# Segment sums on one Trainium2 core: additions two products behind their matmuls, with PSUM banks redistributed

## The chip, the cores and the metric

The kernel runs on one core of a Trainium2 chip. The metric is the device time of one launch in microseconds. Nine runs before the change have a median of 2163.39 us (2159.84 to 2167.46).

The engines are named as in the profile: PE is TensorE, DVE VectorE, ACT ScalarE, POOL GpSimd, and SP is the engine whose queue issues most DMA transfers. PEld is PE's loading of weights.

## The reference

A graph layer with a residual and a layer norm. There are 6250 nodes and 206250 edges, all with 128 features in float32.

```python
edge_aggr = zeros((n, 128)).at[src].add(edge_attr)          # 206250 rows into 6250
combined  = concat([x, edge_aggr, repeat(global_feat, n)]) @ W_c + b_c
h = softplus(combined @ W1 + b1)
h = softplus(h @ W2 + b2)
out = layernorm(x + h @ W3 + b3)                            # no scale or shift
```

`src` is not sorted. Nearly all of the time goes to the scatter-add in the first line.

## The kernel before, in words

**The data.** An edge's row of 128 numbers lies on one partition, and 128 edges, one a partition, make a column: 1611 whole columns and one of 42 edges. The node sums are kept transposed in one tile, `sums_t`: 128 features on the partitions, 25 blocks of 256 nodes (`BL`) along the row.

**Two ways to add.** The first 48 columns (`DIRECT`) are added directly. ACT compares an edge's node with 512 node numbers at a time (`compare`, L535, two columns a step, tile `direct_hot`). PE multiplies the rows with these comparisons into the PSUM tile `direct_sum` (L552). After 12 columns DVE adds the bank to `sums_t` (L556).

All other edges go through buckets, in ten groups (`GROUPS`) of 40, 120, 200, 240, 240, 240, 212, 140, 88 and 44 columns. Each group has four stages:

- *Positions* (`positions`, L236): each edge gets a row in a DRAM table (`place`) in which edges of one node block lie together. A block's bucket is padded to whole chunks. DVE, PE and PSUM work this out: `count` and `count2` count edges by block (PSUM tile `small`, L261), `totals` makes bucket starts, `scan` counts along a partition, `place` sums it across partitions on PE (PSUM tile `pr`, L325 to L331), `place2` turns it into positions (L340, L342), and `chunk_map` writes each chunk's block as an offset (`offs`, L360).
- *Scatter* (`scatter_rows`, L601): SP loads pieces of ten columns (`rows`, five buffers, loaded three pieces ahead), ACT writes each edge's node number into its 129th element (`code_rows`, L599), and POOL scatters one column at a time with an indirect DMA (L607): 1564 of them.
- *Fill* (`fill_rows`): SP overwrites the table with -1 rows beforehand, so that padding matches no node.
- *Sums* (`reduce_steps`, L384): SP loads 1024 bucket rows at a time (`load`, tile `chunks`). DVE compares their node numbers with 256 numbers in one instruction (`match`, L406, tile `hot`). PE multiplies rows with comparisons (`total`, L421), 128 by 256, into a PSUM tile `part` of two sums. DVE adds each sum into `sums_t` at an offset that it has read into a register (L413 reads, L426 adds). A product, in the sense of this text, fills one `part` tile. A load makes four products in groups 0 and 9 (one row tile a sum), two in groups 1, 7 and 8 (two row tiles a sum) and one in the others (four).

**The order.** While group g is scattered, the sums of group g-1, the positions of group g+1 and the fill for group g+1 are done. Each engine's order is the order in which the Python code calls (a manual schedule for PE, DVE, ACT and SP), and every engine takes its instructions in that order. All SP transfers are in one order as well. For each piece the loop from L659 on issues a row load, a copy and ten scatters, and then as many steps of four lists as are due (`prep`, `sums`, `other`, `filled`): `AHEAD` says at which share of a group's pieces each list must be empty. `other` holds the node rows: `node_rows` (L443) turns x with PE (L489) and multiplies it by folded weights (L497), all of it during group 3, with two `x_sb` buffers. The direct steps are spread over groups 1 to 6 by `left` (L653).

In `reduce_steps`, step i loads chunk i+2, compares chunk i and then does the products and additions of chunk i-1. There are four chunk buffers, two comparison buffers and two `part` banks. The eight PSUM banks before are: one for `iota_ps`, two `small`, two `pr`, two `part`, one `direct_sum`.

**The end.** After the last group's scatter its sums are made (L689), and then two softplus layers, the last layer and the layer norm run over 13 tiles of up to 512 nodes (L702 on), with x loaded again by SP and b3 added to it on POOL (L796).

## Time and profile before

| | |
|---|---|
| median of nine runs | 2163.39 us |
| the profiled execution | 2164.55 us, span 2162.8 us |
| granted PE clock, mean | 0.917 |
| PE busy | 1766.1 us (82%) |
| DVE busy | 1383.4 us (64%) |
| ACT busy | 815.3 us (38%) |
| POOL busy | 1554.7 us (72%) |
| scatters (L607) | 1564, mean 958 ns, first at 26.6 us, last at 2006.0 us |
| matmuls of the bucket sums (L421) | 4472, mean 393 ns |
| comparisons of the buckets (L406) | 281, mean 2268 ns |
| additions (L426) | 781, mean 420 ns |

A span runs from the first to the last instruction; the profiled execution's own time is 1.75 us more. Times in the rows of the profile are microseconds from the span's start unless they are marked ns. "A <- B" in a list of waits means that A stood idle until B was done; the three numbers are the total, how often, and the longest. Register and semaphore instructions do not count as busy, and matmul ends are modelled. A float32 matmul shows as two instructions.

### The profile page before, as it was taken

The numbers are of one execution on the slowest core, as the hardware profiler recorded it, in microseconds if no ns is written. First come the engines' busy times: TensorE is split into PE (matmuls) and PEld (weight loads), VectorE is DVE, ScalarE is ACT, GpSimd is POOL, SyncE is SP. The second block draws the span as 40 slices with busy tenths as digits, with TensorE's granted clock in tenths as the row PEclk, the third lists the DMA queues.
The fourth block names the chain that finished last, engine by engine and source line by source line (L and its number), as shares of the span: only waits on it lengthen the run. The fifth ranks groups of instructions, "written<-read, shape, count | busy, mean of one in ns | idle before, by whom it ended". The sixth has DMA issues, their size and how long they took to land.

```text
span 2162.8 us, 22153 instructions
## 1 busy us (share of the span) xinstructions
PE 1766.1 (82%) x6415; PEld 1185.4 (55%) x6415; DVE 1383.4 (64%) x1943; ACT 815.3 (38%) x1174; POOL 1554.7 (72%) x1631
## 2 busy tenths in 40 slices
PE   3399798957999959999769998499983898688885
PEld 0144355534666636666446665276762777567653
DVE  7386476424777537776347764277662788798867
ACT  0367675652444444545443554443430000000035
POOL 5677777777777777777777777777777777777026
PEclk8699898977999979999979999799996999899997
DMA  9998788738888656566466555465654777777421
GB/s 291 303 323 268 211 252 251 241 101 255 240 255 237 179 149 216 189 207 209 131 184 202 185 180 183 133 207 193 202 185 147 213 229 228 199 215 204 122 77 60
DMA packets 415375, 435.49 MB, mean 201 GB/s; under 512 B 37743, under 2 KB 305766, under 8 KB 415254
## 3 DMA queue, kind: packets, MB, share of 16 engines
q1 hardware_dynamic: 365062, 330.71, 52.4%
q0 software_dynamic: 50048, 103.35, 14.3%
q8 instruction: 51, 0.84, 0.2%
q14 instruction: 70, 0.57, 0.1%
q10 hardware_dynamic: 144, 0.02, 0.0%
HBM read 260.90 MB, written 173.03 MB: 201 GB/s over the span
## 4 chain that ended last, share of the span: by engine, by line
PE 39%; POOL 18%; DMA 17%; issue 11%; DVE 10%; ACT 2%; SPq 2%; DVEq 0%; POOLq 0%; ACTq 0%
PE part L421 22%; POOL place L607 18%; PE direct_sum L552 13%; DMA place<-rows,pos 9%; DMA chunks<-place 4%; DVE sums_t L426 4%; DVE hot L406 2%; SPq L143 2%; DMA x_sb<-in_x 2%; DMA place<-fill 2%; DVE so_far L309 1%; DMA rows<-in_edge_attr 1%; PE pr L331 1%; ACT direct_hot L540 1%; PE small L266 1%
## 5 line engine op out<-in xcount | busy, mean ns | idle before, releaser
L607 POOL DMA_INDIRECT place<-rows,pos x1564 | 1497.9, 958 | 501.9 <-issue 445.8
L421 PE MATMUL part<-hot,chunks 128*128 128x256 f32 x4472 | 1062.2, 393 | 201.7 <-DVE hot L406 169.0
L421 PEld LDWEIGHTS part<-hot,chunks 128*128 128x128 f32 x4472 | 863.7, 196 | 421.7 <-DVE hot L406 187.0
L406 DVE SCALAR_TENSOR_TENSOR hot<-chunks,iota_ps 128x2048 f32<-128x2048 f32 (+1 forms) x281 | 637.1, 2268 | 259.9 <-DMA chunks<-place 259.9
L540 ACT ACTIVATE direct_hot<-iota_f,less 128x512 f32<-128x512 f32 (+1 forms) x624 | 405.1, 696 | 674.0 <-PE direct_sum L552 671.6
L552 PE MATMUL direct_sum<-direct_hot,direct_rows 128*128 128x512 f32 (+1 forms) x1248 | 581.6, 599 | 66.0 <-DMA direct_rows<-in_edge_attr 27.1
L426 DVE TENSOR_TENSOR sums_t<-sums_t,part 128x256 f32 x781 | 327.8, 420 | 334.6 <-PE part L421 313.0
L552 PEld LDWEIGHTS direct_sum<-direct_hot,direct_rows 128*128 128x128 f32 x1248 | 239.4, 196 | 284.6 <-issue 228.8
L542 ACT ACTIVATE direct_hot<-direct_hot,ones 128x1024 f32<-128x1024 f32 (+1 forms) x312 | 348.1, 1116 | 10.1
L599 ACT COPY rows<-low 128x10 f32<-128x10 f32 (+1 forms) x159 | 31.3, 199 | 514.9 <-DMA place<-rows,pos 474.6
L342 DVE TENSOR_REDUCE pos<-at 128x20 int32<-128x500 f32 (+2 forms) x80 | 87.1, 1089 | 2.7
L309 DVE TENSOR_TENSOR_SCAN so_far<-iota_ps,ib 128x1500 bf16<-128x1500 f32 (+5 forms) x29 | 85.7, 2955 | 0.0
L556 DVE TENSOR_TENSOR sums_t<-sums_t,direct_sum 128x512 f32<-128x512 f32 (+1 forms) x52 | 34.6, 666 | 66.7 <-PE direct_sum L552 65.9
L796 POOL TENSOR_TENSOR x_sb<-x_sb,b_all 128x512 f32<-128x512 f32 (+1 forms) x13 | 15.3, 1221 | 80.9 <-DMA x_sb<-in_x 80.9
L340 DVE TENSOR_TENSOR at<-pr,ib 128x500 f32<-128x500 f32 (+2 forms) x80 | 52.8, 659 | 3.0 <-PE pr L331 2.4
L721 ACT ACTIVATE away<-z_ps 128x512 f32<-128x512 f32 (+1 forms) x13 | 7.2, 554 | 120.3 <-PE z_ps L711 120.3
L784 POOL TENSOR_SCALAR y<-y,mv,rs 128x128 f32<-128x128 f32 (+1 forms) x45 | 35.1, 792 | 17.2 <-DVE rs L778 17.0
L255 DVE TENSOR_TENSOR ib<-block,iota_ps 128x1500 bf16<-128x1500 bf16 (+5 forms) x29 | 44.3, 1550 | 0.0
L266 PE MATMUL small<-ib,ones_h 128*128 128x500 bf16 (+2 forms) x80 | 24.2, 412 | 24.0 <-DVE ib L255 24.0
L327 PE MATMUL pr<-so_far,ones_h 128*128 128x500 bf16 (+2 forms) x80 | 32.2, 402 | 13.5 <-DVE last L312 13.5
L326 PE MATMUL pr<-ib,upto_h 128*128 128x500 bf16 (+2 forms) x80 | 32.1, 402 | 9.6 <-DVE at L340 9.6
L331 PE MATMUL pr<-begin,scale_h 2*128 2x500 bf16 (+2 forms) x80 | 32.6, 407 | 0.0
(113 smaller groups left out, 415.7 us busy)
## 6 DMA issues: line engine op xcount, KB each, us to landing
chunks<-place SPq DMA_DIRECT2D x278, 516.0 KB, 5.7
rows<-in_edge_attr SPq DMA_DIRECT2D x155, 640.0 KB, 5.1
place<-fill SPq DMA_DIRECT2D x252, 258.0 KB, 8.1
place<-rows,pos POOLq DMA_INDIRECT x1564, 4.3
x_sb<-in_x SPq DMA_DIRECT2D x24, 256.0 KB, 4.6
direct_rows<-in_edge_attr SPq DMA_DIRECT2D x4, 768.0 KB, 7.9
out<-y SPq DMA_DIRECT2D x12, 256.0 KB, 2.2
chunks<-place SPq DMA_DIRECT2D x3, 258.0 KB
```

Of the source, the lines that this page charges most:

```text
L266: nc.tensor.matmul(got["sum"][:, :, :j1 - j0], ones_h, in_block[k][1][:, :, j0:j1], start=(k == 0 and j0 == 0), stop=(k == len(parts) - 1 ...
L309: nc.vector.tensor_tensor_scan(t, iota_ps[:, 1:2].to_broadcast([P, NB * n]), in_block[k][0], 0.0, op0=ALU.mult, op1=ALU.add)
L331: nc.tensor.matmul(pr, scale_h, got["begin"].unsqueeze(2).to_broadcast([2, NB, m]), start=False, stop=True)
L340: nc.vector.tensor_mul(at, got.pop((k, j0)), in_block[k][1][:, :, j0:j1])
L342: nc.vector.tensor_reduce(pos[:, a - c0 + j0:a - c0 + j1], at.rearrange("p b g -> p g b"), axis=mybir.AxisListType.X, op=ALU.add)
L406: nc.vector.scalar_tensor_tensor(hot[:, :m], chunks[i][:, :m, D:W].to_broadcast([P, m, BL]), float(1 + BL * g), iota_ps.unsqueeze(1).to_br ...
L421: nc.tensor.matmul(part[:, s - q, :], t[:, s * sub + j, :D], hot[:, s * sub + j], start=(j == 0), stop=(j == sub - 1))
L426: nc.vector.tensor_add(here, here, part[:, s - q, :])
L540: nc.scalar.activation(hot[:, j, :n], iota_f[:, :n], AF.Abs, bias=less[:, w, c + q + j:c + q + j + 1], scale=-1.0)
L542: nc.scalar.activation(hot[:, :, :n], hot[:, :, :n], AF.Relu, bias=ones[:, :1], scale=-1.0)
L552: nc.tensor.matmul(sum_of[c, w][:, :n], rows_in[c][:, q + j, :], hot[:, j, :n], start=(q + j == 0), stop=(q + j == k - 1))
L607: s = nc.gpsimd.indirect_dma_start(out=dst, out_offset=bass.IndirectOffsetOnAxis(ap=at, axis=0), in_=rows[:r, j, :], in_offset=None)
```

## The change

- `reduce_steps`: `total` is split into `product` (matmuls of one `part` tile) and `add` (its additions). Step i loads chunk i+3, compares chunk i, and issues chunk i's products at once; after each product the oldest waiting additions are issued until only two products wait (`SUMS` - 1). The register load of a chunk's offsets stands before the chunk's first addition. A last step issues what still waits. There are three `part` banks, three comparison buffers (`hots`) and five chunk buffers.
- `place` takes its PSUM tile from the two banks of `small`; the `pr` tile is gone.
- The direct sums have two `direct_sum` banks and four `direct_hot` buffers.
- `low` (node numbers) lies in the memory of `src_i`.
- The node rows are spread over groups 3, 4 and 5, and within each between 80% and 95% of its pieces; `left` takes off 9 columns in each of these groups where it took off 26 in group 3.

```diff
@@ -34,7 +34,9 @@
 PART_COLS = 60
 
 
-AHEAD = (0.75, 0.95, 0.9, 0.75)
+AHEAD = (0.75, 0.95, None, 0.75)
+
+SUMS = 3
 
 LEAD = 3
 
@@ -168,9 +170,9 @@
         per = phase.enter_context(tc.tile_pool(name="per", bufs=2))
         hots_p = phase.enter_context(tc.tile_pool(name="in_block", bufs=4))
         rows_p = phase.enter_context(tc.tile_pool(name="rows", bufs=LEAD + 2))
-        chunks_p = phase.enter_context(tc.tile_pool(name="chunks", bufs=4))
+        chunks_p = phase.enter_context(tc.tile_pool(name="chunks", bufs=5))
         direct_p = phase.enter_context(tc.tile_pool(name="direct", bufs=1))
-        hots = phase.enter_context(tc.tile_pool(name="hots", bufs=2))
+        hots = phase.enter_context(tc.tile_pool(name="hots", bufs=3))
         ps = phase.enter_context(tc.tile_pool(name="ps", bufs=1, space=PSUM))
 
         iota_ps = ps.tile([P, BL], F32, name="iota_ps")
@@ -178,7 +180,8 @@
 
         src_i = keep.tile([P, TC], I32, name="src_i")
         block = keep.tile([P, TC], BF16, name="block")
-        low = keep.tile([P, TC], F32, name="low")
+
+        low = src_i.bitcast(F32)
         chunk_i = keep.tile([NB, NSC_MAX], F32, name="chunk_i")
         fill = keep.tile([P, FILL * W], F32, name="fill")
 
@@ -322,7 +325,8 @@
 
             def place(k, j0, j1):
                 m = j1 - j0
-                pr = by_col(ps.tile([P, 512], F32, name="pr", bufs=2))[:, :, :m]
+                pr = by_col(ps.tile([P, 4, P], F32, name="small", bufs=2)
+                            .rearrange("p a b -> p (a b)"))[:, :, :m]
                 nc.tensor.matmul(pr, upto_h, in_block[k][1][:, :, j0:j1], start=True, stop=False)
                 nc.tensor.matmul(pr, ones_h, so_far[k][:, :, j0:j1], start=False, stop=False)
                 nc.tensor.matmul(
@@ -408,36 +412,56 @@
                     float(1 + BL * g), iota_ps.unsqueeze(1).to_broadcast([P, m, BL]),
                     op0=ALU.subtract, op1=ALU.is_equal)
 
-            def total(i):
+            at_of = {}
+            pending = []
+
+            def product(i, q):
+                k = loads[i][1]
+                t, hot = chunks[i], hot_of[i]
+                part = ps.tile([P, 2, BL], F32, name="part", bufs=SUMS)
+                for s in range(q, min(k, q + 2)):
+                    for j in range(sub):
+                        nc.tensor.matmul(part[:, s - q, :], t[:, s * sub + j, :D],
+                                         hot[:, s * sub + j],
+                                         start=(j == 0), stop=(j == sub - 1))
+                if q + 2 >= k:
+                    del chunks[i], hot_of[i]
+                pending.append((i, q, part))
+
+            def add():
+                i, q, part = pending.pop(0)
                 s0, k = loads[i]
-                _, at = nc.values_load_multi_w_load_instructions(
-                    offs_of[g][:, s0:s0 + k], engines=[DVE], min_val=0, max_val=(NB - 1) * BL,
-                    skip_runtime_bounds_check_because="it is held under the last block")
-                t, hot = chunks.pop(i), hot_of.pop(i)
-                for q in range(0, k, 2):
-                    part = ps.tile([P, 2, BL], F32, name="part", bufs=2)
-                    for s in range(q, min(k, q + 2)):
-                        for j in range(sub):
-                            nc.tensor.matmul(part[:, s - q, :], t[:, s * sub + j, :D],
-                                             hot[:, s * sub + j],
-                                             start=(j == 0), stop=(j == sub - 1))
-                    for s in range(q, min(k, q + 2)):
-                        here = sums_t[:, bass.ds(at[s], BL)]
-                        nc.vector.tensor_add(here, here, part[:, s - q, :])
+                if q == 0:
+                    _, at_of[i] = nc.values_load_multi_w_load_instructions(
+                        offs_of[g][:, s0:s0 + k], engines=[DVE], min_val=0,
+                        max_val=(NB - 1) * BL,
+                        skip_runtime_bounds_check_because="it is held under the last block")
+                for s in range(q, min(k, q + 2)):
+                    here = sums_t[:, bass.ds(at_of[i][s], BL)]
+                    nc.vector.tensor_add(here, here, part[:, s - q, :])
+                if q + 2 >= k:
+                    del at_of[i]
 
             steps = []
             n = len(loads)
-            for i in range(min(2, n)):
+            for i in range(min(3, n)):
                 steps.append(lambda i=i: load(i))
-            for i in range(n + 1):
+            for i in range(n):
                 def one(i=i):
-                    if i + 2 < n:
-                        load(i + 2)
-                    if i < n:
-                        match(i)
-                    if i:
-                        total(i - 1)
+                    if i + 3 < n:
+                        load(i + 3)
+                    match(i)
+                    for q in range(0, loads[i][1], 2):
+                        product(i, q)
+
+                        while len(pending) > SUMS - 1:
+                            add()
                 steps.append(one)
+
+            def end():
+                while pending:
+                    add()
+            steps.append(end)
             return steps
 
         def node_rows():
@@ -534,7 +558,7 @@
 
             def compare(c, w, q):
                 n = min(WIDE, NB * BL - w * WIDE)
-                hot = direct_p.tile([P, QUAD, WIDE], F32, name="direct_hot", bufs=3)
+                hot = direct_p.tile([P, QUAD, WIDE], F32, name="direct_hot", bufs=4)
                 hot_of[c, w, q] = hot
                 for j in range(QUAD):
                     nc.scalar.activation(hot[:, j, :n], iota_f[:, :n], AF.Abs,
@@ -547,7 +571,7 @@
                 k = min(SET, ND - c)
                 hot = hot_of.pop((c, w, q))
                 if q == 0:
-                    sum_of[c, w] = ps.tile([P, WIDE], F32, name="direct_sum", bufs=1)
+                    sum_of[c, w] = ps.tile([P, WIDE], F32, name="direct_sum", bufs=2)
                 for j in range(QUAD):
                     nc.tensor.matmul(sum_of[c, w][:, :n], rows_in[c][:, q + j, :], hot[:, j, :n],
                                      start=(q + j == 0), stop=(q + j == k - 1))
@@ -653,16 +677,23 @@
             left = [0.0] * G
             for g in range(1, G - 3):
                 left[g] = max(0.0, groups[g][1] - groups[g][0]
-                              - groups[g - 1][3] * groups[g - 1][2] / 3 - (26 if g == 3 else 0))
+                              - groups[g - 1][3] * groups[g - 1][2] / 3 - (9 if 3 <= g < 6 else 0))
             direct_at = 0.0
             i = 0
+            assert G > 6
+            nodes = []
             for g in range(G):
                 mine = [q for q in range(len(pieces)) if pieces[q][0] == g]
                 prep = []
                 if g + 1 < G:
                     prep = [lambda g=g: node_codes(*groups[g + 1][:2])] + positions(g + 1)
                 sums = reduce_steps(g - 1) if g else []
-                other = node_rows() if g == min(3, G - 1) else []
+
+                if g == 3:
+                    nodes = node_rows()
+                other = nodes[:-(-len(nodes) // (6 - g))] if 3 <= g < 6 else []
+                if 3 <= g < 6:
+                    nodes = nodes[len(other):]
                 filled = fill_rows(g + 1)
                 done = [0, 0, 0, 0]
                 for q in mine:
@@ -673,7 +704,12 @@
 
                     now = []
                     for w, todo in enumerate((prep, sums, other, filled)):
-                        share = min(1.0, (q - mine[0] + 1) / (AHEAD[w] * len(mine)))
+                        share = (q - mine[0] + 1) / len(mine)
+                        if w == 2:
+                            share = (share - 0.8) / 0.15
+                        else:
+                            share = share / AHEAD[w]
+                        share = max(0.0, min(1.0, share))
                         upto = int(round(len(todo) * share))
                         now.append(todo[done[w]:upto])
                         done[w] = upto
```

## The prediction

> **What bounds the kernel now.** I read the time per stage first, then the waits of POOL, then the DVE and PE rows after POOL's last scatter. The busy shares alone mislead: PE shows 82%, POOL 72%. The stretches say more (columns: busy time with instruction counts for PE, PEld, DVE, ACT and POOL, then PE clock, DMA share and GB/s):
>
> ```profile
> 26.00:2007.00 1981.00, 1649.95 (x5994) 1112.04 (x5994) 1246.24 (x1580) 765.96 (x1091) 1497.94 (x1564) 0.92 0.70 210
> 2007.00:2031.00 24.00, 22.33 (x96) 17.75 (x96) 21.02 (x30) 0.00 (x0) 0.00 (x0) 1.00 0.50 134
> 2031.00:2086.00 55.00, 39.42 (x136) 26.71 (x136) 46.88 (x79) 0.00 (x0) 0.00 (x0) 0.91 0.21 54
> 2086.00:2163.00 77.00, 48.86 (x176) 27.66 (x176) 51.48 (x203) 47.57 (x78) 50.33 (x58) 0.83 0.28 83
> ```
>
> All 1564 scatters lie in the first row. 1981 us / 1564 = 1.267 us each; one is 0.96 us, and the 0.30 us behind it is called "issue". POOL's waits:
>
> ```profile
> POOL place L607 <- issue: 445.8, 1462, 0.3
> POOL place L607 <- DMA w_sb<-in_L_gnn_W: 19.5, 1, 19.5
> POOL place L607 <- DMA place<-rows,pos: 17.1, 56, 0.3
> POOL place L607 <- DMA rows<-in_edge_attr: 6.7, 3, 6.1
> ```
>
> Only two entries are real waits: 19.5 us before the first scatter and 6.1 us once among the early rows. Everything else is that same 0.3 us gap, whatever releaser the profile names. So from 26.6 to 2007 us POOL walks at its own pace and PE, DVE and ACT have only to keep up. The chain of waits gives PE 39% because it follows what ended last at each hop; those PE pieces lie in POOL's shadow.
>
> Behind POOL comes DVE. The last two groups' sums run from 1959.68 us (when the first chunk of group 8 has landed) to 2086.2 us. In the DVE timeline (start, duration, count, and in brackets idle time and releaser) this is the end of group 8 and the start of group 9:
>
> ```profile
> 2023.75 2.28 DVE L406 SCALAR_TENSOR_TENSOR hot<-chunks,iota_ps 128x2048 f32<-128x2048 f32 x1
> 2025.95 1.85 DVE L426 TENSOR_TENSOR sums_t<-sums_t,part 128x256 f32 x4
> 2028.90 0.88 DVE L426 TENSOR_TENSOR sums_t<-sums_t,part 128x256 f32 x2 [1.11 <-PE part L421]
> 2030.63 0.87 DVE L426 TENSOR_TENSOR sums_t<-sums_t,part 128x256 f32 x2 [0.85 <-PE part L421]
> 2031.42 4.48 DVE L406 SCALAR_TENSOR_TENSOR hot<-chunks,iota_ps 128x2048 f32<-128x2048 f32 x2
> 2035.82 1.89 DVE L426 TENSOR_TENSOR sums_t<-sums_t,part 128x256 f32 x4
> 2038.71 1.86 DVE L426 TENSOR_TENSOR sums_t<-sums_t,part 128x256 f32 x4 [1.00 <-PE part L421]
> 2040.49 2.28 DVE L406 SCALAR_TENSOR_TENSOR hot<-chunks,iota_ps 128x2048 f32<-128x2048 f32 x1
> 2042.68 1.85 DVE L426 TENSOR_TENSOR sums_t<-sums_t,part 128x256 f32 x4
> 2044.78 1.86 DVE L426 TENSOR_TENSOR sums_t<-sums_t,part 128x256 f32 x4 [0.24 <-PE part L421]
> 2046.55 2.28 DVE L406 SCALAR_TENSOR_TENSOR hot<-chunks,iota_ps 128x2048 f32<-128x2048 f32 x1
> ```
>
> A load of group 9 costs 2046.55 - 2040.49 = 6.06 us, a load of group 8 3.96 us (its comparisons start at 2019.79 and 2023.75), and DVE is at work in nearly all of it. Past 2007 us DVE's waits on PE total only 1.96 us (in the rows of 2028.90 and 2030.63) plus 5.3 us in group 9.
>
> **The change part by part.**
>
> *Mid-run parts at nothing.* Third PSUM bank and comparison buffer, loads three ahead, second bank for the direct sums, fourth direct comparison, positions on the "small" banks, node rows spread over groups 3 to 5: until 1959 us all serve work hidden by POOL. ACT's 671.6 us wait for the direct sums and DVE's 259.9 us for chunks shrink unpaid. The cover is the lead of the coded rows over their scatter: smallest after the start is the copy ended at 560.60 for the scatter at 588.21, 27.6 us. Positions are ready well ahead too (group 9's at 1924.2, needed at 1951.7). SP's order barely moves: a chunk load three ahead waits for the product two loads back, as one two ahead with one buffer fewer did, and that product now stands one step earlier on PE. The row loads queued behind it are therefore not held longer. Ends for the mid-run: 0, and the stall priced below.
>
> *Positions on two shared banks* adds a wait: a product's PE instructions now stand directly behind their comparison, so the count's total on DVE can stand behind a whole product, 3.7 us (16 PE instructions in 3.72 us), once or twice a group, with prep's rest behind it. Group 7's sums must end by 1959.68; they ended 0.64 us before. They also contain 8.6 us of DVE waiting on PE, partly removable. Ends: 0 and 3 us later; I take 0, as the landing of group 8's rows, unmoved, then ends last.
>
> *Group 8, two row tiles a chunk.* A load has two products, so two behind is one load behind: comparison, register load, four additions, the same DVE order as now. No gain per load. Only the end differs: with a third bank PE need not wait for load 15's additions before it starts load 16. The last product is ready some 6.3 us after the comparison's start (2.28 + two products of 1.86 + 0.2), against 2030.63 - 2023.75 = 6.88: **-0.6 us**.
>
> *Group 9, one tile a chunk.* A load has four products, so additions lag half a load. DVE's order becomes comparison, four additions, register load, four additions. Today the register load comes with the comparison and runs under it. Now it stands between additions. From the chain of waits:
>
> ```profile
> 2046.21 0.42 DVE sums_t L426
> 2046.64 0.24 DVEq L413
> 2046.88 0.14 DVE hot L406
> ...
> 2047.23 1.52 issue
> ```
>
> The load of eight offsets ends 0.67 us after the last addition's start; with the small register steps behind it the next addition could start about 0.95 us after it, where 0.52 is usual: 0.43 exposed. Four additions without a wait take 4 x 0.49 = 1.96 us, against 2044.78 - 2042.68 = 2.10 now, so 0.14 goes. Net +0.29 a load, x8: **+2.3 us**. Ends: +0.8 (0.24 exposed, the idle time at 2084.34 where a register load already stands between additions) and +4.0 (0.5, nothing recovered).
>
> The Trainium skill, "DMA: Bandwidth & Descriptors", section "Latency and other measured facts", gives a tensor load a floor of about 600 ns, which speaks against putting it between additions; the row has 0.67 for eight offsets, so by the page the term would be eight times about 0.05 us smaller.
>
> *Start of group 9.* Now two comparisons, then 1.00 us idle. After, one comparison (2.28), then idle until its first product ends 1.1 us later plus latency: 1.3 us. **+0.3 us**.
>
> *Slow products.* PE rows of two successive loads:
>
> ```profile
> 2069.07 4.21 PE L421 MATMUL part<-hot,chunks 128*128 128x256 f32 x16 [1.85 <-DVE sums_t L426]
> 2075.13 5.42 PE L421 MATMUL part<-hot,chunks 128*128 128x256 f32 x16 [1.85 <-DVE sums_t L426]
> ```
>
> The second is 1.2 us longer at the same shape: part of it ran at a reduced clock (0.91 granted in this stretch, 1.00 in the one before). DVE's waits there are 0.43 and 0.86, and 0.73 and 0.83 after 2063, instead of 0.24 a load: 2.85 - 0.48 = 2.4 us. With additions two products behind, a product may be about 0.8 us late unseen, so I take them as absorbed: **-2.4 us**; ends -2.4 and 0.
>
> The Trainium skill, "TensorE: Matmul & The Clock Gate", section "Why this matters for your kernels", asks for no PE gaps above about 3 us. Here gaps of 1.85 us go with reduced clock. By the page alone the slow products would vanish and the term stand whole; by the rows they recur and it rests on the slack.
>
> *Dense layers:* same instructions; their node-row loads wait for the last register load, which stays about 2 us before the last addition. 0.
>
> Sum: -0.6 + 2.3 + 0.3 - 2.4 = -0.4 us. The profiled execution took 2164.55 us (span 2162.8), 1.2 above the median of 2163.39; against the median the prediction is **2163.0 us**. Ends: -0.6 + 0.8 + 0 - 2.4 = -2.2 and 0 + 4.0 + 1.3 + 0 + 3 (group 7) = +8.3. A measurement of this kernel tells about 0.2%, 4.3 us, from no change.
>
> **The rivals.**
>
> 1. *The tail gains.* DVE's waits after 2007 us (7.3 us) all vanish and the register loads hide. Against: they follow an addition that waits for the one before it, so they can't start earlier. Price: -7.3 + 1.3 (first product) = -6: 2157.4 us.
>
> 2. *Register loads are fully exposed and slow products remain*, the sum's upper ends without group 7: +4.0 + 1.3 = +5.3; 2168.7 us, slower. It decides if a load of group 9 takes over 6.5 us instead of 6.06. Against: 0.67 is the measured length.
>
> 3. *PE falls behind and POOL starves*, slower. Four or five node-row steps now share 15% of a 303 us group, 45 us, each on a load of 4.6 us median (10.64 at worst in the chain). All exposed: 5 x 10.6 = 53 us of PE. It decides beyond the rows' lead, 37.7 us at least in group 4: 15 us lost in each of two or three groups, 2193 us or more. Against: only 11.4 us of PE's waits are on these loads today.
>
> 4. *The change speeds the sums and nothing pays*: that is the forecast.
>
> **How the numbers follow.** Forecast 0.82, rival 1 0.08, rival 2 0.07, rival 3 0.03. Within 0.2% 0.82, faster 0.08, slower 0.10. The range 2158.5 to 2168.5 reaches to rivals 1 and 2; beyond it lie rival 3 and the outer halves of those two.
>
> **What would show it.** Right: POOL's scatters still 1.26 us apart, the last at about 2006 us; ACT's wait for the direct sums far shorter; group 9's loads 6.3 us apart with two addition runs of four, a gap of about 0.4 us at the register load, and few waits on PE. Wrong: a scatter waiting for rows or positions; group 8's first comparison after 1960 us; loads of group 9 below 6.0 or above 6.5 us.

## The result and the profile after

The changed kernel takes 2172.82 us (median of ten runs, 2171.44 to 2185.45). The kernel before has a median of 2163.95 us over 31 runs. The ratio is 1.0057, 95% interval 1.0044 to 1.0070: slower by about half a percent, and outside the predicted range of 2158.5 to 2168.5 us.

The profiled execution took 2172.8 us with a span of 2171.0 us, 8.2 us more than the span before. These are its stretches in four stages, cut as before (PE, PEld, DVE, ACT and POOL busy, PE clock, DMA share, GB/s):

```profile
25.00:2015.00 1990.00, 1677.75 (x6010) 1137.58 (x6010) 1235.24 (x1587) 761.92 (x1091) 1498.05 (x1564) 0.93 0.73 209
2015.00:2036.00 21.00, 18.91 (x82) 14.79 (x80) 18.90 (x30) 0.00 (x0) 0.00 (x0) 1.00 0.51 135
2036.00:2092.00 56.00, 38.22 (x136) 27.66 (x136) 46.50 (x78) 0.00 (x0) 0.00 (x0) 0.91 0.18 44
2092.00:2171.00 79.00, 50.36 (x176) 27.63 (x176) 51.28 (x203) 47.65 (x78) 50.30 (x58) 0.81 0.27 81
```

The first stage has grown. The last scatter starts at 2013.77 us instead of 2006.02. POOL's waits name one releaser that was absent before:

```profile
POOL place L631 <- issue: 449.2, 1473, 0.3
POOL place L631 <- DMA cols<-in_L_gnn_b: 18.3, 1, 18.3
POOL place L631 <- ACT rows L623: 10.5, 4, 7.0
POOL place L631 <- DMA rows<-in_edge_attr: 5.9, 2, 5.5
```

So the scatters have waited for coded rows. The wait is short, but it shows that the cover the prediction relied on, the lead of a piece's code copy over its first scatter, is gone. Worked out from the trace, the least lead is now 8.0 us in group 3 (27.6 before), 0.27 in group 4 (37.7), 0.57 in group 5 (39.2) and 0.27 in group 6 (40.0). POOL loses time at 807.8 us (6.7 us) and at 1429.2 us (2.6 us). This is the first of these in the timeline (start, duration, engine, and in brackets idle time and releaser):

```profile
783.84 0.19 ACT L623 COPY rows<-src_i 128x10 f32<-128x10 f32 x1
791.78 1.34 ACT L564 ACTIVATE direct_hot<-iota_f,less 128x512 f32<-128x512 f32 x2 [7.74 <-PE direct_sum L576]
799.83 0.96 POOL L631 DMA_INDIRECT place<-rows,pos  x1 [0.30 <-issue]
802.32 1.33 ACT L564 ACTIVATE direct_hot<-iota_f,less 128x512 f32<-128x512 f32 x2 [8.02 <-PE direct_sum L576]
807.32 0.19 ACT L623 COPY rows<-src_i 128x10 f32<-128x10 f32 x1
807.78 0.96 POOL L631 DMA_INDIRECT place<-rows,pos  x1 [6.99 <-ACT rows L623]
```

A code copy takes 0.19 us. It is late because in ACT's order it stands behind direct comparisons, and these wait for PE's direct products: 7.74 and 8.02 us here. So PE is behind, and ACT hands that on to POOL.

Why PE is behind shows in the waits of group 3 (486 to 789 us). The changed kernel first, then the kernel before:

```profile
ACT direct_hot L564 <- PE direct_sum L576: 178.2, 39, 12.8
DVE sums_t L580 <- PE direct_sum L576: 100.2, 8, 15.2
PE part L424 <- DVE hot L410: 73.0, 14, 26.0
```

```profile
ACT direct_hot L540 <- PE direct_sum L552: 171.5, 42, 21.2
DVE sums_t L426 <- PE part L421: 56.0, 28, 4.7
DVE sums_t L556 <- PE direct_sum L552: 5.6, 6, 2.7
PE part L421 <- DVE hot L406: 0.7, 1, 0.7
```

DVE now stands 100.2 us at the addition of a direct sum instead of 5.6. PE stands 73.0 us waiting for bucket comparisons, which it hardly did before (0.7 us). A wait of DVE alone need not cost anything, and much of this one has only moved: over the whole span DVE's waits rose from 65.9 to 408.4 us at the direct additions, but fell from 313.0 to 75.0 at the bucket additions and from 259.9 to 46.1 for chunks. What is new is that PE waits in return, 269.5 us for comparisons over the span instead of 169.0. The two engines wait for each other in turn. One round of it, from the timeline of the changed kernel:

```profile
635.04 3.72 PE L424 MATMUL part<-hot,chunks 128*128 128x256 f32 x16
638.60 1.88 PE L576 MATMUL direct_sum<-direct_hot,direct_rows 128*128 128x512 f32 x4
640.52 0.69 DVE L580 TENSOR_TENSOR sums_t<-sums_t,direct_sum 128x512 f32<-128x512 f32 x1 [13.59 <-PE direct_sum L576]
642.87 2.27 DVE L410 SCALAR_TENSOR_TENSOR hot<-chunks,iota_ps 128x2048 f32<-128x2048 f32 x1
645.19 5.88 PE L424 MATMUL part<-hot,chunks 128*128 128x256 f32 x16 [4.71 <-DVE hot L410]
```

DVE stands 13.59 us at the direct addition, until PE has worked off everything queued ahead of that sum. The next comparison is behind the addition on DVE. PE's next products are directly behind that comparison, so PE, once it has caught up, has nothing to do for 4.71 us. The kernel before did the products of chunk i-1 in step i, so a chunk compared a step earlier was in hand at this point.

**The tail.** This is DVE at the end of group 8 and the start of group 9:

```profile
2033.43 0.88 DVE L441 TENSOR_TENSOR sums_t<-sums_t,part 128x256 f32 x2 [0.32 <-PE part L424]
2035.16 0.88 DVE L441 TENSOR_TENSOR sums_t<-sums_t,part 128x256 f32 x2 [0.85 <-PE part L424]
2035.95 2.28 DVE L410 SCALAR_TENSOR_TENSOR hot<-chunks,iota_ps 128x2048 f32<-128x2048 f32 x1
2042.41 2.28 DVE L410 SCALAR_TENSOR_TENSOR hot<-chunks,iota_ps 128x2048 f32<-128x2048 f32 x1
2044.61 1.85 DVE L441 TENSOR_TENSOR sums_t<-sums_t,part 128x256 f32 x4
2046.91 1.86 DVE L441 TENSOR_TENSOR sums_t<-sums_t,part 128x256 f32 x4 [0.45 <-PE part L424]
2048.68 2.28 DVE L410 SCALAR_TENSOR_TENSOR hot<-chunks,iota_ps 128x2048 f32<-128x2048 f32 x1
```

A load of group 9 takes 6.27 us (2048.68 - 2042.41), 6.06 before. The 0.45 us idle is where the register load stands. The profile names a product there, but this gap goes when the register load is moved, as shown below. From the last scatter to the last addition it is 78.37 us, 80.18 before. The dense layers behind it take 78.87 us, 76.57 before, at the same instructions. Their first PE rows show why; the changed kernel, then the kernel before:

```profile
2092.79 1.30 PE L746 MATMUL z_ps<-z_x,ident 128*128 128x512 f32 x2
2093.89 1.91 PE L747 MATMUL z_ps<-sums_t,fold 128*128 128x512 f32 x2
2095.59 1.65 PE L746 MATMUL z_ps<-z_x,ident 128*128 128x512 f32 x2
```

```profile
2086.84 1.04 PE L710 MATMUL z_ps<-z_x,ident 128*128 128x512 f32 x2
2087.72 1.02 PE L711 MATMUL z_ps<-sums_t,fold 128*128 128x512 f32 x2
2088.58 1.02 PE L710 MATMUL z_ps<-z_x,ident 128*128 128x512 f32 x2
```

The same matmuls take up to 1.9 times as long: the trace grants half the clock from 2093.44 us on for 3.41 us, just there.

The 8.24 us of span add up: -1.14 to the first scatter, -0.58 to the first scatter of group 1, +9.47 from there to the last scatter, -1.81 to the last addition, +2.30 for the dense layers.

### The profile page after: what moved, and what is told of

It is laid out like the page before. It is cut to its first block, busy times and chain, and to the rows that moved or that the text cites. A ratio compares the mean times of both kernels' runs of the same rounds, so it can differ in the third digit from the quotient of the medians.

```text
span 2171.0 us, 22052 instructions
## 1 busy us (share of the span) xinstructions
PE 1790.8 (82%) x6415; PEld 1209.0 (56%) x6415; DVE 1368.5 (63%) x1943; ACT 811.4 (37%) x1174; POOL 1554.8 (72%) x1631
## 4 chain that ended last, share of the span: by engine, by line
PE 58%; DVE 20%; DMA 7%; issue 7%; POOL 4%; ACT 2%; SPq 1%; DVEq 1%; POOLq 0%; ACTq 0%
PE part L424 37%; PE direct_sum L576 16%; DVE hot L410 8%; POOL place L631 4%; DVE sums_t L441 4%; DMA place<-fill 3%; DMA place<-rows,pos 2%; DVE so_far L312 2%; DVE sums_t L580 1%; SPq L145 1%; DVE pos L346 1%; PE small L335 1%; DMA chunks<-place 1%; DMA rows<-in_edge_attr 1%; DVE at L344 1%
## 5 line engine op out<-in xcount | busy, mean ns | idle before, releaser
L424 PE MATMUL part<-hot,chunks 128*128 128x256 f32 x4472 | 1107.7, 405 | 272.3 <-DVE hot L410 269.5
L424 PEld LDWEIGHTS part<-hot,chunks 128*128 128x128 f32 x4472 | 894.8, 203 | 513.8 <-DVE hot L410 337.8
L564 ACT ACTIVATE direct_hot<-iota_f,less 128x512 f32<-128x512 f32 (+1 forms) x624 | 404.6, 695 | 806.2 <-PE direct_sum L576 802.4
L410 DVE SCALAR_TENSOR_TENSOR hot<-chunks,iota_ps 128x2048 f32<-128x2048 f32 (+1 forms) x281 | 636.6, 2267 | 46.1 <-DMA chunks<-place 46.1
L576 PE MATMUL direct_sum<-direct_hot,direct_rows 128*128 128x512 f32 (+1 forms) x1248 | 559.0, 581 | 29.5 <-DMA direct_rows<-in_edge_attr 25.7
L576 PEld LDWEIGHTS direct_sum<-direct_hot,direct_rows 128*128 128x128 f32 x1248 | 233.4, 190 | 232.1 <-issue 204.5
L580 DVE TENSOR_TENSOR sums_t<-sums_t,direct_sum 128x512 f32<-128x512 f32 (+1 forms) x52 | 34.7, 667 | 408.4 <-PE direct_sum L576 408.4
L623 ACT COPY rows<-src_i 128x10 f32<-128x10 f32 (+1 forms) x159 | 30.8, 196 | 394.6 <-DMA place<-rows,pos 348.2
L832 POOL TENSOR_TENSOR x_sb<-x_sb,b_all 128x512 f32<-128x512 f32 (+1 forms) x13 | 15.2, 1206 | 78.9 <-DMA x_sb<-in_x 78.9
L344 DVE TENSOR_TENSOR at<-small,ib 128x500 f32<-128x500 f32 (+2 forms) x80 | 52.8, 660 | 4.3 <-PE small L335 3.6
L523 DVE TENSOR_SCALAR z_x<-small,z_bias 128x512 f32<-128x512 f32 (+1 forms) x13 | 9.3, 717 | 51.3 <-PE small L521 51.3
L331 PE MATMUL small<-so_far,ones_h 128*128 128x500 bf16 (+2 forms) x80 | 31.5, 393 | 11.1 <-DVE last L315 11.1
L285 DVE TENSOR_REDUCE size_f<-small 128x25 f32<-128x500 f32 x10 | 6.8, 677 | 50.1 <-PE small L269 50.0
```

The costliest lines, as they stand in the source:

```text
L344: nc.vector.tensor_mul(at, got.pop((k, j0)), in_block[k][1][:, :, j0:j1])
L410: nc.vector.scalar_tensor_tensor(hot[:, :m], chunks[i][:, :m, D:W].to_broadcast([P, m, BL]), float(1 + BL * g), iota_ps.unsqueeze(1).to_br ...
L424: nc.tensor.matmul(part[:, s - q, :], t[:, s * sub + j, :D], hot[:, s * sub + j], start=(j == 0), stop=(j == sub - 1))
L564: nc.scalar.activation(hot[:, j, :n], iota_f[:, :n], AF.Abs, bias=less[:, w, c + q + j:c + q + j + 1], scale=-1.0)
L576: nc.tensor.matmul(sum_of[c, w][:, :n], rows_in[c][:, q + j, :], hot[:, j, :n], start=(q + j == 0), stop=(q + j == k - 1))
L580: nc.vector.tensor_add(here, here, sum_of.pop((c, w))[:, :n])
```

## The experiments

Two theories. *Order*: the products' place directly behind their comparison makes PE and DVE wait for each other at the direct additions, and the rows' lead is spent on that. *Node rows*: squeezed into 80 to 95% of groups 3 to 5, they hold up PE and SP there and so the rows. The runs fell on two sorts of chip. On one the kernel before takes about 2170 us, much like the chip of the result. On the other it takes about 2860 us, TensorE paces the kernel, and POOL waits for rows for hundreds of us whatever the kernel. Only the first sort answers the question; the second has a paragraph of its own.

### On chips where the kernel before takes about 2170 us

**The changed kernel again** (no edit).

> The changed kernel once more, beside three variants of it on one chip, since the last four runs came from a chip on which the kernel before took 2852 us and TensorE's matmuls came in stretches at a third of their rate. On a chip where the kernel before takes about 2164 us: 2172 us again (ratio 1.004 to 1.007). On a chip like the last: the order theory (each direct addition stands ahead of a comparison, and products stand directly behind their comparison) expects a ratio near that of the kernel without node rows there, 1.003 to 1.012, since TensorE is the bound there and each of its waits counts; the node-row theory expects about 1.000, as its stalls of the scatters drown there.

2178.8 us against 2171.1: ratio 1.0040 (1.0025 to 1.0056). Least lead 0.27 us again. The result holds in a second set of runs.

**The changed kernel without node rows** (`z_x` is set to 0 instead, so the result lacks the part of x):

```diff
-            for b0 in range(0, -(-N // P), 4):
-                steps.append(lambda b0=b0: turn(b0))
-                steps.append(lambda b0=b0: first(b0))
```

> The changed kernel with the node rows' loads, transposes, copies and first products left out (so z_x stays zero and the node rows of the result are wrong). On a chip where the kernel before takes about 2164 us: the order theory alone expects the rows' lead in groups 3 to 6 to fall as in the changed kernel and scatters to stall, 2168 to 2173; the node-row theory expects no stall, 2160 to 2165; if it takes both, the lead falls to below 20 us inside the groups but does not reach zero, and the time is 2162 to 2166. On a slow chip: ratio 1.007 to before as measured there.

2169.4 us, ratio 0.9988 (0.9979 to 0.9996). The waits stay: DVE 437.2 us at the direct additions (405.7 in the changed kernel beside it, 65.9 before), PE 278.0 us for comparisons. The lead still falls, to 8.9 us in group 3, but does not reach zero, and no scatter stalls. So the order spends the lead and the node rows take what is left. This run leaves out the work of the node rows and not only their new place; their place alone is the last run of this part.

**The changed kernel with the direct addition issued four job steps later:**

```diff
                 if q + QUAD == k:
+                    owed.append((c, w, n))
+                if owed and (q == 3 * QUAD or (c, w, q) == jobs[-1]):
+                    c, w, n = owed.pop(0)
                     here = sums_t[:, w * WIDE:w * WIDE + n]
                     nc.vector.tensor_add(here, here, sum_of.pop((c, w))[:, :n])
```

> The changed kernel with VectorE's addition of a direct sum issued four job steps later, inside the next window. On a chip where the kernel before takes about 2164 us: the order theory expects VectorE's waits at the direct addition to fall from 408 us to below 100, TensorE's for comparisons from 270 us to below 150, and 2162 to 2167 us, the tail unchanged. The node-row theory expects 2170 to 2174. On a slow chip: ratio 0.992 to before as measured there.

2169.1 us, ratio 0.9995 (0.9987 to 1.0004). DVE waits 15.9 us at these additions. The lead stays at 20.4 us or more with the node rows where the change put them, and no scatter stalls. PE still waits 246.3 us for comparisons, not below the 150 expected: with products directly behind their comparison it arrives early. The scatters lose nothing by that wait here.

**The changed kernel with products one step behind their comparison**, as in the kernel before, and everything else of the change kept:

```diff
-            for i in range(n):
+            for i in range(n + 1):
...
-                    match(i)
-                    for q in range(0, loads[i][1], 2):
-                        product(i, q)
+                    if i < n:
+                        match(i)
+                    for q in range(0, loads[i - 1][1] if i else 0, 2):
+                        product(i - 1, q)
```

> The changed kernel with the products of a load issued one step after its comparison. On a chip where the kernel before takes about 2164 us: the order theory expects TensorE's waits for comparisons to fall from 270 us to below 120 although VectorE still stands at its direct additions, and no stall of the scatters, so that what is left is the tail: 2161 to 2167 us. The node-row theory expects 2170 to 2174. On a slow chip: ratio 0.989 to before as measured there.

2164.75 us, ratio 0.9971 (0.9961 to 0.9981): 14 us less than the changed kernel on the same chip and faster than the kernel before. The least lead in groups 3 to 6 is 37.6 us. Its waits over the span:

```profile
DVE sums_t L581 <- PE direct_sum L577: 199.0, 46, 11.5
PE part L424 <- DVE hot L410: 137.8, 8, 43.4
```

DVE still stands 199 us at the direct additions, but PE's wait for comparisons has gone down to eight occasions (137.8 us in all, where below 120 was expected). The same place as above in this kernel:

```profile
638.01 3.72 PE L424 MATMUL part<-hot,chunks 128*128 128x256 f32 x16
641.57 1.88 PE L577 MATMUL direct_sum<-direct_hot,direct_rows 128*128 128x512 f32 x4
643.29 3.62 PE L424 MATMUL part<-hot,chunks 128*128 128x256 f32 x16
643.49 0.69 DVE L581 TENSOR_TENSOR sums_t<-sums_t,direct_sum 128x512 f32<-128x512 f32 x1 [1.05 <-PE direct_sum L577]
```

PE passes from the direct products straight on to a product whose comparison is long done. DVE's stand no longer reaches it.

**The kernel before with the new order alone**: products directly behind their comparison and additions one product behind, with its own banks, buffers and node rows (`...` stands for `total` split into `product` and `add`, and for a last step that issues what still waits, as in the change):

```diff
...
-            for i in range(n + 1):
+            for i in range(n):
                 def one(i=i):
                     if i + 2 < n:
                         load(i + 2)
-                    if i < n:
-                        match(i)
-                    if i:
-                        total(i - 1)
+                    match(i)
+                    for q in range(0, loads[i][1], 2):
+                        product(i, q)
+
+                        while len(pending) > 1:
+                            add()
...
```

> The kernel before with each load's products issued directly behind their comparison and additions one product behind, all else as before, on a chip where the kernel before takes about 2165 us. Order theory: VectorE's wait at the direct additions rises from 66 us to over 250, TensorE's for comparisons from 169 us to over 230; the lead falls below 15 us and in group 3, with the node rows, may reach zero; ratio 1.001 to 1.030. Rival: lead above 22 us, ratio 0.998 to 1.002.

2299.5 us, ratio 1.0593 (1.0578 to 1.0608), twice the loss that was thought possible. Its waits:

```profile
PE part L420 <- DVE hot L406: 336.2, 136, 10.8
DVE sums_t L576 <- PE direct_sum L572: 268.4, 51, 10.2
POOL place L627 <- ACT rows L619: 88.1, 21, 10.4
```

The lead is at 0.27 us in groups 3, 4 and 5. The tail has grown too: the sums of group 8 start 39.0 us after the first scatter of group 9 (7.9 before) and take 5.16 us a load (3.96 before), so that the sums end 127.9 us after the last scatter instead of 80.2. Within the change, the rest of it (a third bank and comparison buffer, loads three ahead, a second direct bank) brings the loss down from 5.9% to 0.57%; without the order it gains 0.3%, as the kernel with products a step later shows. Which part of it pays most was not tried.

**The kernel before with the new place of the node rows alone:**

```diff
-AHEAD = (0.75, 0.95, 0.9, 0.75)
+AHEAD = (0.75, 0.95, None, 0.75)
...
+                        if w == 2:
+                            share = (share - 0.8) / 0.15
...
```

Here `...` stands for the steps spread over groups 3 to 5 and for the 9 columns that `left` takes off in each of them, as in the change.

> The kernel before with the node rows alone moved to 80 to 95% of groups 3 to 5. On a chip where the kernel before takes about 2165 us: with the order theory the least lead of the coded rows in groups 3 to 6 stays above 20 us (27.6 before; 37.6 with the products one step behind and these node rows), no stall of scatters, ratio 0.998 to 1.002. If the node rows stall by themselves: lead near zero at the end of group 3 or the start of group 4 and ratio 1.002 or more. On a slower chip: 0.99 to 1.02, which tells nothing.

2171.1 us against 2169.4: ratio 1.0002 (0.9992 to 1.0011). The least lead in groups 3 to 6 is 31.3 us and no scatter stalls. On this sort of chip the node rows do no harm by themselves. Putting them back into group 3 within the changed kernel was not tried.

The runs of this sort side by side. "Main" is from the first scatter of group 1 to the last scatter, "sums" from there to the last addition, "dense" the rest (us, one profiled execution each):

| kernel | least lead, groups 3-6 | main | sums | dense | ratio |
|---|---|---|---|---|---|
| before | 27.6 | 1922.9 | 80.2 | 76.6 | 1 |
| changed | 0.27 | 1932.3 | 78.4 | 78.9 | 1.0057 |
| changed, run again | 0.27 | 1930.9 | 78.4 | 78.8 | 1.0040 |
| without node rows | 8.9 | 1923.8 | 80.3 | 78.7 | 0.9988 |
| direct addition late | 20.4 | 1923.1 | 78.6 | 78.9 | 0.9995 |
| products a step later | 37.6 | 1924.0 | 77.4 | 76.7 | 0.9971 |
| order alone | 0.27 | 2012.4 | 127.9 | 77.2 | 1.0593 |
| node rows alone | 31.3 | 1923.8 | 78.2 | 76.6 | 1.0002 |

### The register load by itself

The prediction's largest term of the tail was the register load between additions. First it was issued ahead of the next comparison (with the products one step behind):

```diff
+                    if i:
+                        where(i - 1)
                     if i < n:
                         match(i)
```

> The changed kernel with the products one step behind their comparison, and VectorE's register load of the offsets issued ahead of the next comparison instead of between additions. It measures the register load's term by itself. If the load costs 0.45 us where it stands (the idle time seen there in the last group), the loads of group 9 come 5.82 to 5.9 us apart instead of 6.27, the tail behind the last scatter is 2.5 to 3.2 us shorter than the 154.1 us without the hoist, and the ratio to before is about 0.0013 lower: 0.9955 to 0.9962. Rival: the wait is really the product's, and stays when the load is gone: loads 6.2 to 6.3 us apart and a ratio of 0.997 as without the hoist.

This fell on the slower sort of chip (ratio 1.0009, 0.9947 to 1.0072), but DVE's rows in group 9 can be read all the same:

```profile
2721.31 3.81 DVE L443 TENSOR_TENSOR sums_t<-sums_t,part 128x256 f32 x8
2725.40 2.29 DVE L410 SCALAR_TENSOR_TENSOR hot<-chunks,iota_ps 128x2048 f32<-128x2048 f32 x1 [0.28 <-issue]
2727.61 3.81 DVE L443 TENSOR_TENSOR sums_t<-sums_t,part 128x256 f32 x8
```

Neither side was right. The gap between additions has gone (eight run through), but 0.28 us has come up ahead of the comparison, and a load takes 6.29 us. The register load is 0.60 us long in the trace. It starts with the addition ahead of it, which takes 0.42 us, and the comparison starts only after it. The next edit puts it behind the comparison of 2.28 us, where the kernel before has it (against the edit above):

```diff
-                    if i:
-                        where(i - 1)
                     if i < n:
                         match(i)
+                    if i:
+                        where(i - 1)
```

> The changed kernel with the products one step behind their comparison and the register load of the offsets issued right behind the next comparison, ahead of all additions. If the register load (0.60 us long) hides under the comparison (2.28 us), loads of group 9 come 5.82 to 5.95 us apart (2.20 for the comparison, eight additions 3.9 us, less the overlap seen) instead of 6.27 to 6.29, and the tail behind the last scatter is 2 to 3 us shorter than with the products' order alone: ratio 0.9955 to 0.9965 where the kernel before takes about 2165 us, against 0.9971 without this step. If DVE pays for a register load wherever it stands: 6.2 to 6.3 us apart and 0.997.

> The changed kernel with the products one step behind their comparison and the register load right behind the next comparison, on a chip where the kernel before takes about 2165 us: loads of group 9 5.92 us apart, as measured on the slower chip, against 6.27; eight such loads make 2.5 us, so ratio 0.9955 to 0.9965 against 0.9971 with the register load between additions. If the reduced clock falls on the dense layers' first products (2.2 us longer, as in the changed kernel), 0.9965 to 0.998.

On the slower chip 2834.1 us, ratio 0.9951 (0.9909 to 0.9994), loads 5.92 us apart. On a chip where the kernel before takes 2169.7 us: 2162.4 us, ratio 0.9964 (0.9952 to 0.9976), the best version here. Its rows there:

```profile
2052.78 2.28 DVE L410 SCALAR_TENSOR_TENSOR hot<-chunks,iota_ps 128x2048 f32<-128x2048 f32 x1
2054.97 3.81 DVE L443 TENSOR_TENSOR sums_t<-sums_t,part 128x256 f32 x8
2058.70 2.28 DVE L410 SCALAR_TENSOR_TENSOR hot<-chunks,iota_ps 128x2048 f32<-128x2048 f32 x1
```

5.92 us a load. The register load starts with the last addition here too (2058.38 us), but the comparison no longer waits for it: it starts 0.34 us after that addition's start, against 0.70 with the register load ahead of it. So the register load costs 0.35 us a load between additions (6.27 - 5.92), 0.37 us ahead of the comparison (6.29 - 5.92) and nothing behind it. The idle times in the rows, 0.45 and 0.28 us, are not these costs: 0.10 us of the first stands at such places without a register load too, and a comparison otherwise starts 0.08 us before the addition ahead of it has ended.

The sums end 74.2 us after the last scatter, 3.2 less than with the register load between additions (77.4); 2.2 of these lie in group 9 (51.67 us from its first comparison to its last addition, against 53.84). The two medians were measured beside different runs of the kernel before, and the intervals of their ratios overlap, so only the rows show the step.

### On chips where the kernel before takes about 2860 us

The first four runs, and those below, met TensorE in another condition. These rows are 128x256 products of the kernel with products a step later; the first row has 13 of them, 0.21 us apart:

```profile
906.37 2.97 PE L424 MATMUL part<-hot,chunks 128*128 128x256 f32 x13
910.23 0.38 PE L424 MATMUL part<-hot,chunks 128*128 128x256 f32 x1 [0.89 <-issue]
911.66 0.38 PE L424 MATMUL part<-hot,chunks 128*128 128x256 f32 x1 [1.05 <-issue]
913.76 0.59 PE L424 MATMUL part<-hot,chunks 128*128 128x256 f32 x1 [1.72 <-issue]
```

Then, for some ten us, PE's matmuls start 1.4 to 2.1 us apart with nothing to wait for that the profile shows. The mean granted clock is 0.82 to 0.84 here, against 0.92 to 0.94. In the kernel with the node rows alone moved, PE is busy 1920.4 us on such a chip and 1760.3 us on the other sort, and stands idle for 260 us (0 on the other) without a releaser; the busy times of DVE, ACT and POOL agree within 1%.

> The changed kernel with the node rows' turns and products left out (z_x is set to 0 instead, so the first layer lacks the part of x). Theory A (each direct addition on DVE waits for PE, the next comparison stands behind it, and PE's products stand directly behind the comparison, so PE loses ground in groups 3 to 6): the lead of the coded rows still falls to about 20 us inside group 3, DVE still waits about 400 us for the direct sums, and there is still some stall of POOL at group starts; 2166 to 2172 us. Theory B (the node rows, put into the last fifth of groups 3 to 5, hold PE and SP there): no stall of POOL, about 2165 us, and leads above 30 us. If the two only starve POOL together: 2165 us with leads near 20 us.

> The changed kernel, but DVE adds a finished direct sum only after the fourth comparison pair of the next window has been multiplied, so that the addition's product is long done when DVE comes to it. Theory A: DVE's wait for the direct sums falls from 408 us to below 50, PE's wait for comparisons from 270 us to about 170, the rows' lead stays above 30 us, POOL does not stall: about 2164 to 2165 us. Theory B: DVE's waits move elsewhere and the stalls at the starts of groups 4 and 6 stay: about 2172 us.

> The changed kernel, but the products of a chunk are issued a step after its comparison, as before the change; three banks, additions two products behind and everything else stay. Theory A: PE has a whole chunk's products in hand while DVE waits and compares, PE's wait for comparisons falls to about 170 us, no stall: about 2164 to 2166 us. Theory B: no difference to the changed kernel, about 2172 us. Group 9 should take as long a load as in the changed kernel, 6.27 us, or less.

> The kernel before with the new place of the node rows (80 to 95% of groups 3 to 5, and the new share of direct steps) and nothing else. Theory A: the rows' lead dips at the ends of groups 3 to 5 but stays above 15 us, no stall: about 2164 us. Theory B: stalls of 4 to 9 us at the starts of groups 4 to 6: 2168 to 2174 us.

The numbers expected were for the other sort of chip. Measured against the kernel before, 2852.6 us: without node rows 1.0066 (1.0024 to 1.0109), direct addition late 0.9924 (0.9886 to 0.9961), products a step later 0.9885 (0.9849 to 0.9921), node rows alone 0.9978 (0.9918 to 1.0037). Where TensorE paces the kernel the order counts directly, with no lead to spend first: even with its node-row work left out the changed order loses, and either way out of the lockstep wins about 1%.

> The kernel before with the node rows alone moved to 80 to 95% of groups 3 to 5. Order theory (node rows harm only where the changed order has used up the rows' lead): lead at the ends of groups 3 to 5 falls to 15 to 30 us, no stall of the scatters, ratio 0.998 to 1.002. Node-row theory (they stall the rows by themselves): stalls of 5 us or more at the start of group 4 or 5, ratio 1.003 or more.

> The kernel before with one thing changed: each load's products issued directly behind their comparison, additions one product behind; two banks, two comparison buffers, one direct bank, loads two ahead, positions' own banks and node rows as they were. Order theory: VectorE's wait at the direct additions rises from 66 us to over 250, TensorE's for comparisons from 169 us to over 230, the least lead of the coded rows in groups 3 to 6 falls from 27.6 us to below 15 us, and the ratio is 1.001 to 1.010, by whether the lead reaches zero. Rival (the extra wait comes from three loads ahead or from the shared banks, not from the order): lead above 22 us, waits near those of before, ratio 0.998 to 1.002.

> The kernel before with the node rows alone moved to 80 to 95% of groups 3 to 5, on a chip where the kernel before takes about 2165 us. Order theory: lead of the coded rows at the ends of groups 3 to 5 falls to 15 to 30 us, no stall of the scatters, ratio 0.998 to 1.002. Node-row theory: stalls of 5 us or more, ratio 1.003 or more.

> The kernel before with each load's products issued directly behind their comparison and additions one product behind, all else as before, on a chip where the kernel before takes about 2165 us. Order theory: VectorE's wait at the direct additions rises from 66 us to over 250, TensorE's for comparisons from 169 us to over 230; the lead falls below 15 us; ratio 1.001 to 1.030, since on the chip with the slower TensorE this kernel took 4.6% longer than before. Rival: lead above 22 us, ratio 0.998 to 1.002.

The order alone: 1.0460 (1.0410 to 1.0510) and 1.0496 (1.0431 to 1.0562). The node rows alone: 1.0079 (1.0031 to 1.0126) and 1.0127 (1.0063 to 1.0192), which does not agree with the 0.9978 above; what they cost on such chips stays open.

## Why the prediction was wrong

**The step that failed is "mid-run parts at nothing".** It put at 0 what measured +9.47 us from the first scatter of group 1 to the last scatter, 9.3 of them in two stalls of POOL for coded rows. Its cover was named rightly, the lead of 27.6 us. Its reason was not: the product "now stands one step earlier on PE" was taken for a help to SP's loads. It is the loss of PE's work in hand. A product one step behind its comparison can run while DVE stands elsewhere; a product directly behind it can't. The order alone costs 5.9%, and with the rest of the change it is 0.57%. Nothing in the profile of before showed a wait there, since it was the old order that kept it small: 65.9 us for DVE at the direct additions. The prediction said ACT's wait for direct sums would shrink; it rose from 671.6 to 802.4 us.

**Rival 3** had the outcome in kind (PE falls behind, POOL starves) with the wrong cause and price. It blamed the node rows at 15 us a group. They are only the last push: alone they cost nothing on this sort of chip, and the two stalls lost 6.7 and 2.6 us.

**The range.** The sum's own upper end was +8.3 us, 2171.7, but the stated range stopped at 2168.5, at rival 2, which leaves the 3 us of group 7 out. That +8.3 comes near the measured +8.9 is luck: it was made up of the tail and of group 7, and the loss lay in two stalls of the scatters, early in groups 4 and 6.

**The tail**, -0.4 us predicted, came to +0.5 (-1.81 + 2.30), from terms that did not match:

- *Register load*, +0.29 a load: 0.21 (6.27 against 6.06). The mechanism was right. The addition behind the register load starts 0.87 us after the one ahead of it, where 0.52 is usual, so 0.35 us is exposed and not 0.43. The floor of about 600 ns that the Trainium skill gives for a tensor load ("DMA: Bandwidth & Descriptors", section "Latency and other measured facts") is near the 0.60 us of these eight offsets, but it is no floor here: in group 8, loads of four offsets last 0.34 us.
- *Start of group 9*, +0.3: start and end of the group together cost 1.1 us more than before. The first load took 6.46 us, with a stretch of half clock on its first product; when the kernel was run again, without one there, it took 5.28.
- *Slow products*, -2.4: they cost about 2.1 us in two loads before (7.27 and 7.00 us against 6.06) and 0.7 after (6.65 and 6.62 against 6.27), so -1.4. "Absorbed" was mostly right.
- *Group 8*, -0.6: -0.93 from its first comparison to that of group 9 (70.81 us against 71.74).
- *Positions' shared banks*, "the landing of group 8's rows, unmoved, then ends last": it moved. SP issued the first chunk loads of group 8 1.2 us after the first scatter of group 9, against 3.5 before, and its first comparison came 5.66 us after that scatter against 7.94. That is -2.28 us that the prediction did not have; what moved it was not tried.
- *Group 9* as a whole took 56.19 us from its first comparison to its last addition, against 54.78: +1.41 where the terms give +0.2 (+1.7 for the register loads, -1.4 for slow products and +1.1 for start and end). It varies: when the kernel was run again it took 54.61.
- *Dense layers*, 0: +2.30. A stretch of half clock, 3.41 us long, met the first dense products, where nothing hides it. It did so in all four executions with the changed order and three banks (78.7 to 78.9 us). With products a step later it did not (76.7), nor with the order alone (77.2). PE's idle time ahead of the dense layers is 1.92 us in the changed kernel and 2.00 with products a step later, so its length alone doesn't decide it; what does is open. In all these traces the stretches start whole multiples of 3.41 us apart. The idle time ahead of the dense layers lies inside one such step in the four executions, and across two with products a step later; but in the sums of the changed kernel 1.95 us of idle time inside one step brought no stretch, and 1.69 us did. The Trainium skill's rule of no PE gaps above about 3 us ("TensorE: Matmul & The Clock Gate", section "Why this matters for your kernels") doesn't tell these cases apart either.

Of the signs listed, "a scatter waiting for rows" and "group 8's first comparison after 1960 us" (1965.1) came, and the loads of group 9 with no stretch of half clock on them took 6.27 to 6.34 us, between 6.0 and 6.5 as expected (two with one took 6.62 and 6.65).

## What to carry to other kernels

When an edit moves work of one engine closer behind the engine that feeds it, ask what it had in hand while the feeder stood still, and look for every other wait on the feeder: here one addition in twelve columns was enough. A lead of 30 us is a stock, so price what a change takes from it in each step and not only whether the stock exists. A register load was free here with a long instruction issued ahead of it, and not with a short one.

## What the runs showed of the hardware that was not expected

- The same kernel takes 2164 to 2171 us on some chips and 2853 to 2869 us on others, with scatters of 0.96 us on both. The difference lies in TensorE: stretches in which its matmuls start 1.4 to 2.1 us apart with nothing to wait for that the profile shows. Why is open.
- DVE's register load of eight offsets is 0.60 us long and starts together with an addition of 0.42 us. It costs 0.35 us between two additions, 0.37 us between an addition and a comparison, and nothing when it is issued behind a comparison of 2.28 us.
- In the tails of these kernels the granted clock falls to half for 3.41 us at a time, and such stretches start whole multiples of 3.41 us apart. One falls 0.7 to 1.3 us after the last addition in all four executions with the changed order and three banks.
